# Weight loads on another engine's queue, and other constants in a planner that writes the order of a fused attention and feed-forward block

## The chip, the cores and the metric

The kernel runs on one core of one Trainium2 chip. Engines are named as the profile names them: PE is TensorE (PEld its weight loads), DVE is VectorE, ACT is ScalarE, POOL is GpSimd, SP is SyncE. Times are device microseconds. Three executions before the change took 1146.23, 1144.88 and 1145.27 us: median 1145.27. Less is better.

## The reference

The input x has 2 batches of 1024 tokens with 512 channels. With xn the layer norm of x over its channels:

```python
qkv = einsum('bsd,od->bso', xn, w_qkv) + b_qkv          # 32 heads of 16 channels
scores = q @ k.T / sqrt(16) + slope[head] * position[key]
scores = where(query >= key, scores, -1e9)
s = softmax(scores) @ v ; s = s @ w_out.T + b_out
gate, up = octonion_linear(xn, w_gate), octonion_linear(xn, w_up)    # weights cut to -scale, 0, +scale
g = silu(octonion_linear(silu(gate) * up, w_down))
out = x + s * g
```

An octonion linear layer multiplies 8 slices of the channels by 8 weight blocks, with the signs of an octonion product; the feed-forward part has 8 * 170 = 1360 hidden channels. The 1e9 mask, the softmax over 1024 keys and all sums are in float32.

## The kernel before, in words

The program has two stages. Attention fills the first 868 us of the profiled execution, the feed-forward part (`gate_up`, `down`) the rest; the change touches the first alone.

**Attention.** The 32 heads are worked on in 8 groups of 4, two groups to a pair. The work is cut into 32 *units* (batch, group, half of the queries). A *group (b, g)* below means the two units of batch b and group g. For each unit there are four kinds of steps:
- *Max scores* (`max_items`, L538): PE multiplies 128 queries by up to 512 keys into a tile of the PSUM pool `ps_x`, which has two buffers; DVE adds the mask to the diagonal block and takes the row's maximum. The names are `s1_...` in the program and `s` in the profile.
- *Placing the maxima* (`split_max`, `place_max`, L603): DVE splits the maxima in two parts, PE turns them, ACT copies them to `mr`, and two small DMAs from POOL write them into rows of the query tile `q_stack`, so that the next product subtracts them. The line of POOL is `q_stack<-mr`.
- *Exps* (`exp_step`, `exp_of`, L654 and L673): PE computes transposed scores into one of three buffers of `ps_e`, ACT takes the exponential into the SBUF tile `p`.
- *Values* (`value_step`, L692): PE multiplies `p` by `v`, four heads side by side; ACT copies the sum, PE turns it and DVE divides (`normalise`, L712), SP stores it.

Beside these there is *side work* on PE: projections to queries and keys (`qk_items`, L467), to values (`v_items`, L425), the output projection (`out_items`, L745 and L761) and, early on, transposes of tokens and of the down weights. Its results go through the pool `ps_m`, with two buffers. Queries and keys go out to DRAM and come back in another shape by DMAs of SP (`fill_q`, `fill_k`); they are the tiles `q_stack` and `k_stack`.

**The weights.** `load_wq` fetches the query and key weights of two groups, 512 KB in each of two DMAs, into `wqr`; `compact_wq` copies them together on POOL into `wq`. It is called once at the start and then late in each projection, for the next one (L475 to L477). `load_weight` fetches the gate, up and down weights in three DMAs each; gate was already on POOL, up and down on ACT. The DMAs of SP and of ACT take their completion semaphores in turn from the same eight (the order lists them as DMAHW0 to DMAHW7), those of POOL from eight others (DMASW0 to DMASW7). A DMA whose semaphore is still in use waits at its issue, and what stands behind it on that queue waits too.

**The planner.** `step` (L1261) writes the order of all engines by a list of costs. It keeps a clock for PE (`now`), one each for ACT and DVE (`run_act`, `run_dve`), and the time from which each PSUM buffer is free (`e_free`, `x_free`, `m_free`). `next_max`, `next_exp`, `next_turn`, `next_value`, `next_side` and `next_behind` each offer a next step with the time at which it can start; `step` takes one that can start soon, by priority. Side work has a due position in the units: past it, it has priority 3, before it priority 7, so that it is brought forward when nothing else is ready. Each cost is a number in nanoseconds in the code: from PE's end to the start of ACT or DVE 150, from their end until the buffer can be written again 60, an exp 510, a placing 3500 after ACT's copy. All steps are kept in the order that the planner writes, on every engine; once the attention stage is written, `held.clear()` gives the feed-forward part to the scheduler of the language.

Of the kernel before, what the change touches and what calls it, by code (L numbers as in the profile page):

```python
# [75 lines left out]
def kernel(  # L76
# [132 lines left out]
    act_.activation(warm, ones[:, 0:1], AF.Sqrt)  # L209
    for t in range(8):  # L210
        load_x(t, sp_)
    load_wq((0, 0), act_)
    load_wv(0)
    for n in range(2):
        for i in range(4):
# [235 lines left out]
    def qk_items(b, gp):  # L451

        box = {}

        def product(which, c, kt):
            if (which, c, kt) == (0, 0, 0):
                if (b, gp) not in wq_tiles:
                    compact_wq((b, gp))
                parts[b, gp] = [
                    spill.tile([2, P, S], F32, tag=f"sp{w}", name=f"sp_{b}_{gp}_{w}")  # L460
                    for w in range(2)
                ]
            if kt == 0:
                box["ps"] = ps_m.tile([P, 512], F32, tag="m", name=f"pqk_{b}_{gp}_{which}_{c}")
            ps = box["ps"]
            pe(
                nc.tensor.matmul(  # L467
                    ps,
                    lhsT=wq_tiles[b, gp][:, kt, which, :],
                    rhs=xnT[:, kt, b * S + c * 512 : b * S + (c + 1) * 512],  # L470
                    start=(kt == 0),
                    stop=(kt == KD - 1),
                )
            )
            n = b * NP + gp + 1  # L475
            if (which, c, kt) == (1, n > 1, KD - 1) and n < B * NP:
                load_wq((n // NP, n % NP), act_)  # L477
            if kt < KD - 1:
                return
            bias = bqk_sb[:, which, gp : gp + 1]  # L480
            st = stg.tile([P, 2, 512], F32R, tag="st", name=f"st_{b}_{gp}_{which}_{c}")
            act_.activation(st[:, 0, :], ps, AF.Identity, bias=bias)
            dve_.scalar_tensor_tensor(
                st[:, 1, :], ps, bias, st[:, 0, :].bitcast(F32), ALU.add, ALU.subtract
            )
            sp_.dma_start(
                out=parts[b, gp][which][:, :, c * 512 : (c + 1) * 512].rearrange(
                    "l p n -> p l n"
                ),
                in_=st.bitcast(F32),  # L490
            )

        return [
            (858, lambda w=w, c=c, kt=kt: product(w, c, kt), "qk" if kt == KD - 1 else None)
            for w in range(2)
            for c in range(2)
            for kt in range(KD)
        ]
# [415 lines left out]

    def load_later(w, name):
        later(
            lambda: load_weight(w, name, act_),
            lambda: set_known(("l", name), now[0] + 9000),
            ("k", name),
        )  # L920
# [103 lines left out]
    for t0 in (8, 12):  # L1024
# [18 lines left out]
        ("V", "R"): 200,  # L1043
        ("V", "F"): 100,
    }
    SOON = 80
    RUN = 1800
    HELD = 1e12
# [49 lines left out]
    def next_max(pos):  # L1098
        if M[0] == len(maxs):
            return []  # L1100
        u, n, count, heads_in, cost, diagonal, emit = maxs[M[0]]
        fill = 4 * (u // 2) + 1 + 2 * units[u][2]
        if fills[0] <= fill or n == 0 and u >= 2 and u - 2 not in placed:
            return []

        def go():
            emit()
            M[0] += 1
            run_pe("R", ready, heads_in * max(cost * 0.417 + 18, 108))
            end = run_dve(  # L1110
                now[0] + 150,
                heads_in * cost * 1.04 + 70 + (heads_in * 135 + 70) * diagonal,
            )
            take(x_free)[0] = end + 60
            if n == count - 1:
                split_max(*units[u], mtiles[u])
                turns.append((u, run_dve(end, 500) + 100))

        mpos = at[u] + (at[u + 1] - at[u]) * n / count
        lead = size[1] + size[0] * 0.6  # L1120
        ready = max(fill_at[fill], min(x_free))
        return [(ready, 4 if mpos < pos + lead else 5.5, 0, go)]

    def next_exp():
        if E[0] == len(exps):
            return []
        u, n, i, pieces = exps[E[0]]
        diagonal = n >= 4 * units[u][2]
        if u not in placed or V[0] < cells_at[u] + n - 2:
            return []  # L1130

        def after(ps):
            exp_of(*units[u], n, i, ps)
            end = run_act(now[0] + 150, 510)
            take(e_free)[0] = end + 60
            if i == (3 if len(pieces) == 1 or pieces[0][3] == 384 else 2):
                p_ready[cells_at[u] + n] = end + 60

        def go():
            ps = exp_step(*units[u], n, i, pieces)  # L1140
            E[0] += 1
            cost = sum(max(w * 0.417 + 18, 108) for _, _, _, w in pieces)
            run_pe("R", ready, cost + (60, 120)[len(pieces) - 1] * diagonal)
            after(ps)

        ready = max(placed[u] if n == 0 and i == 0 else 0, min(e_free))
        return [(ready, 5, 0, go)]

    def next_turn():
        found = []  # L1150
        if turns:
            u, t = turns[0]

            def go(u=u):
                turns.pop(0)
                place_max(*units[u], mtiles[u])
                run_pe("F", ready, 436)
                take(m_free)[0] = run_act(now[0] + 150, 500)
                placed[u] = m_free[0] + 3500

            ready = max(t, min(m_free))
            found.append((ready, 1, 0, go))
        if norms:
            u, t = norms[0]

            def go(u=u):
                norms.pop(0)
                normalise(*units[u])
                run_pe("F", t2, 436)
                take(m_free)[0] = run_dve(now[0] + 150, 600)  # L1170
                stored[units[u]] = m_free[0] + 5000

            t2 = max(t, min(m_free))
            found.append((t2, 2, 0, go))
        return [f for f in found if f[0] < HELD]

    def next_value():
        if V[0] == len(vals) or V[0] not in p_ready or not V[0] and S_[0] < head_v:
            return []
        u, n, cell = vals[V[0]]  # L1180
        last = 4 * units[u][2] + 2

        def go():
            value_step(*units[u], n, cell)
            V[0] += 1
            run_pe("V", ready, sum(w * 1.668 + 40 for _, _, w in cell))
            if n == last:
                o_free[0] = run_act(now[0] + 200, 500)
                norms.append((u, o_free[0] + 100))

        ready = max(p_ready[V[0]], o_free[0] if n == 0 else 0)

        if n % 2 == 0 and n < last and V[0] + 2 >= E_cell():
            ready = max(ready, p_ready.get(V[0] + 1, HELD) - 800)
        return [(ready, 0, 0, go)] if ready < HELD else []
# [7 lines left out]
    def next_side(pos):  # L1203
        if S_[0] == len(side):
            return []
        due, ok, (cost, emit, what, *need) = side[S_[0]]
        if not ok():
            return []

        def go():  # L1210
            emit()
            S_[0] += 1
            if cost:
                run_pe("F", ready, cost)
            if what == "none":
                return
            if HELD not in m_free:
                take(m_free)[0] = HELD
            if what is None:
                return  # L1220
            if what == "v":
                end = run_dve(now[0] + 150, 350)
            elif what == "qk":
                end = run_dve(run_act(now[0] + 150, 600), 700)
                done_qk[0] += 1

                if done_qk[0] == 2 or done_qk[0] % 4 == 0:
                    qk_done.append(end + 4000)
            elif what == "t":
                end = run_act(now[0] + 150, 500)  # L1230
            else:
                end = run_dve(now[0] + 150, 600)
            m_free[m_free.index(HELD)] = end + 60

        ready = 0 if HELD in m_free or not cost else min(m_free)
        for k in need:
            ready = max(ready, known[k] + 100)
        return [(ready, 3 if pos >= due else 7, cost, go)]

    def next_behind(pos):  # L1240
# [4 lines left out]
        def go():  # L1245
            behind.pop(0)
            emit()
            if model:
                model()
            if not cost:  # L1250
                return
            run_pe("F", ready, cost)
            if what == "t":
                take(m_free)[0] = run_act(now[0] + 150, 500)

        ready = known.get(need, 0) + 100
        if cost:
# [282 lines left out]
```

## Time and profile before

| | |
|---|---|
| Median of three runs | 1145.27 us |
| Profiled execution | 1146.23 us, of which span 1144.5 us |
| PE busy | 1066.6 us, 93% of the span |
| PEld busy | 702.4 us |
| DVE busy | 678.3 us, 59% |
| ACT busy | 506.7 us, 44% |
| POOL busy | 176.2 us, 15% |
| Granted clock of PE, mean | 0.975 |
| DMA queue q1 (SP and ACT) | 66336 packets, 87.48 MB |
| DMA queue q0 (POOL) | 3776 packets, 5.98 MB |

The chain of work that ended last is 73% PE, 11% DVE, 5% DMA and 4% ACT. A busy PE is not PE at its peak: matmuls are pipelined, their ends are modelled, and a matmul that waits inside its row counts as busy. Issuing a DMA is not counted as busy. A wait for several semaphores is put down to the one that came last. The slices of the page are 28.6 us each.

### The profile page before, as it was taken

How to read it: one execution, taken by the hardware profiler on the slowest of the kernel's cores; microseconds unless marked ns; L12 is line 12 of the kernel's file. 1: busy time of each engine (PE TensorE's matmuls, PEld its weight loads, DVE VectorE, ACT ScalarE, POOL GpSimd, SP SyncE). 2: the span in 40 equal slices, each digit the busy share in tenths (PEclk: the TensorE clock that was granted, in tenths of full speed). 3: DMA queues.
4: the chain of work that ended last, by engine and by line, in shares of the span. 5: the costliest groups of instructions: out<-in, count | busy, mean ns of one | idle time of the engine just before them, and what ended most of it. 6: DMA issues, size and time to landing. Idle time of an engine off the chain costs nothing.

```text
span 1144.5 us, 15617 instructions
## 1 busy us (share of the span) xinstructions
PE 1066.6 (93%) x5562; PEld 702.4 (61%) x5562; DVE 678.3 (59%) x1400; ACT 506.7 (44%) x962; POOL 176.2 (15%) x294
## 2 busy tenths in 40 slices
PE   7889969999998999999999999999879999999995
PEld 5554645675655666556566566565546687878783
DVE  5377786757777687777786877878531122131211
ACT  4122647654653634546536356356662123232321
POOL 6401023000111010100110000010001123242322
PEclk9899968999999999999999999999889999999998
DMA  6976463453745416442645154631041013030200
GB/s 194 204 140 153 108 168 83 59 80 112 145 114 129 72 31 124 130 86 43 138 65 76 66 113 99 137 62 42 17 143 65 33 42 111 1 111 1 77 34 37
DMA packets 73740, 104.24 MB, mean 91 GB/s; under 512 B 26992, under 2 KB 31120, under 8 KB 73664
## 3 DMA queue, kind: packets, MB, share of 16 engines
q1 hardware_dynamic: 66336, 87.48, 34.1%
q10 hardware_dynamic: 3552, 9.78, 2.6%
q0 software_dynamic: 3776, 5.98, 2.1%
q8 instruction: 45, 0.74, 0.3%
q14 instruction: 31, 0.25, 0.1%
HBM read 69.58 MB, written 33.10 MB: 90 GB/s over the span
## 4 chain that ended last, share of the span: by engine, by line
PE 73%; DVE 11%; DMA 5%; ACT 4%; issue 4%; POOL 1%; SPq 0%; ACTq 0%; DVEq 0%; POOLq 0%
PE s L538 13%; PE s L654 12%; PE po L692 11%; PE pg L1375 6%; PE pqk L467 6%; PE pu L1375 6%; PE pd L1409 5%; PE pout L761 4%; DVE mx L69 4%; PE s L673 3%; PE pv L425 3%; DMA q_stack<-mr 2%; DVE s L69 2%; ACT p L69 1%; DVE left L69 1%
## 5 line engine op out<-in xcount | busy, mean ns | idle before, releaser
L69 ACT ACTIVATE p<-s 128x512 f32<-128x512 f32 x576 | 309.9, 600 | 124.6 <-PE s L654 70.0
L538 PE MATMUL s<-k_stack,q_stack 126*128 126x512 f32 (+3 forms) x768 | 279.0, 417 | 24.0 <-DVE mx L69 16.2
L654 PE MATMUL s<-q_stack,k_stack 128*128 128x512 f32 (+3 forms) x768 | 229.0, 367 | 11.3 <-DMA q_stack<-mr 7.7
L69 DVE TENSOR_REDUCE mx<-s 128x1 f32<-128x384 f32 (+3 forms) x352 | 226.3, 643 | 11.7
L69 DVE TENSOR_REDUCE left<-s 128x1 f32<-128x512 f32 x256 | 169.2, 686 | 72.4 <-PE s L538 71.3
L538 PEld LDWEIGHTS s<-k_stack,q_stack 126*128 126x128 f32 x768 | 133.1, 194 | 119.0 <-PE s L538 35.7
L654 PEld LDWEIGHTS s<-q_stack,k_stack 128*128 128x128 f32 x768 | 140.8, 193 | 57.4 <-issue 18.5
L69 DVE TENSOR_TENSOR s<-s,mask 128x128 f32<-128x128 f32 (+2 forms) x352 | 124.2, 353 | 40.3 <-PE s L538 38.6
L692 PE MATMUL po<-p,v 128*32 128x512 f32 (+3 forms) x1536 | 140.5, 494 | 0.2 <-ACT p L69 0.2
L467 PE MATMUL pqk<-xnT,wq 128*128 128x512 f32 x256 | 129.4, 613 | 3.9 <-ACT xnT L69 2.0
L69 DVE SCALAR_TENSOR_TENSOR h<-pu,sc_u,sg 128x512 f32<-128x512 f32 (+1 forms) x44 | 33.0, 751 | 166.8 <-PE pu L1375 154.3
L69 POOL DMA_DIRECT2D q_stack<-mr x64 | 32.0, 505 | 603.3 <-ACT mr L69 603.3
L673 PE MATMUL s<-mask_r,ident_r 128*128 128x256 f32 (+1 forms) x320 | 89.2, 279 | 0.0
L69 POOL TENSOR_TENSOR hs<-h,hs 128x512 fp32r<-128x512 f32 (+1 forms) x44 | 57.5, 1307 | 197.9 <-ACT hs L69 197.8
L692 PEld LDWEIGHTS po<-p,v 128*32 128x32 f32 x1536 | 42.6, 110 | 73.0 <-issue 70.5
L69 ACT ACTIVATE sg<-pg,sc_g 128x512 f32<-128x512 f32 (+1 forms) x44 | 30.2, 687 | 100.5 <-PE pg L1375 95.6
L69 ACT ACTIVATE st<-pqk,bqk_sb 128x512 fp32r<-128x512 f32 x32 | 22.0, 688 | 118.2 <-PE pqk L467 102.3
L425 PE MATMUL pv<-wv,xnT 128*128 128x256 f32 x256 | 68.4, 386 | 1.9 <-DVE v L69 1.5
L467 PEld LDWEIGHTS pqk<-xnT,wq 128*128 128x128 f32 x256 | 48.2, 196 | 32.3 <-issue 22.0
L761 PE MATMUL pout<-wo_sb,oT 128*128 128x512 f32 x128 | 62.0, 606 | 1.4 <-ACT oT L69 1.0
L673 PEld LDWEIGHTS s<-mask_r,ident_r 128*128 128x128 f32 x320 | 60.9, 190 | 2.1
L69 ACT CAST hs<-h 128x512 fp32r<-128x512 f32 (+1 forms) x44 | 27.3, 619 | 75.8 <-DVE h L69 75.8
(143 smaller groups left out, 1100.4 us busy)
## 6 DMA issues: line engine op xcount, KB each, us to landing
sp<-st SPq DMA_DIRECT2D x32, 512.0 KB
k_stack<-sp SPq DMA_DIRECT2D x128, 128.0 KB
q_stack<-sp SPq DMA_DIRECT2D x128, 128.0 KB
wqr<-in_wqk_dram ACTq DMA_DIRECT2D x16, 512.0 KB
xt<-in_x_dram SPq DMA_DIRECT2D x16, 256.0 KB
att<-o SPq DMA_DIRECT2D x32, 128.0 KB
ot<-att SPq DMA_DIRECT2D x16, 256.0 KB
proj<-y SPq DMA_DIRECT2D x16, 256.0 KB
```

The costliest lines, as they stand in the source:

```text
L69: ins = issue(*args, **kwargs)
L425: nc.tensor.matmul(ps[:, 0:256], lhsT=xnT[:, c, b * S + kt * P : b * S + (kt + 1) * P], rhs=wv_tiles[2 * b + hh][:, c, :], start=(c == 0), ...
L467: nc.tensor.matmul(ps, lhsT=wq_tiles[b, gp][:, kt, which, :], rhs=xnT[:, kt, b * S + c * 512 : b * S + (c + 1) * 512], start=(kt == 0), st ...
L538: nc.tensor.matmul(ps[:, j * n : (j + 1) * n], lhsT=q_of(b, g, qc)[0 : NR - 2, first + j, tl * P : (tl + 1) * P], rhs=k_of(b, g, c)[0 : NR ...
L654: nc.tensor.matmul(ps[:, c0 : c0 + w], lhsT=k_of(b, g, kt // 4)[0:NR, h, kt % 4 * P : (kt % 4 + 1) * P], rhs=q[0:NR, h, 512 - w : 512], st ...
L673: pe(nc.tensor.matmul(out, lhsT=ident_r, rhs=rhs, start=False, stop=True))
L692: nc.tensor.matmul(po[32 * i : 32 * i + 32, 512 - w : 512], lhsT=v[:, kt, h * VC : h * VC + 32], rhs=p[:, i * part + c0 : i * part + c0 + ...
L761: nc.tensor.matmul(ps, lhsT=turned[t][:, c, :], rhs=wo_sb[0][:, c, :], start=(c == 0), stop=(c == KD - 1),)
L1375: nc.tensor.matmul(ps[:fs, :], lhsT=fw[mt][:, n0 + kt, 0:fs], rhs=part[:, kt, :], start=(kt == 0 and n == 0), stop=(kt == KD - 1 and n == 1),)
L1409: nc.tensor.matmul(pd, lhsT=hs[k][:fs, n, st * P : (st + 1) * P], rhs=fw[mt][:fs, 8:12, :].rearrange("p s n -> p (s n)"), start=(mt == 0 a ...
```

## The change

The issue of `load_wq` (16 DMAs) and of `load_weight` for up and down (6 DMAs) is moved from ACT to POOL. In the planner the lags from PE to ACT or DVE and back get names, START = 210 (150 before, 200 for the copy of the values' sum) and END = 160 (60 before, 100 after the last maximum of a unit and after the copy of the values' sum); an exp costs 485 in place of 510, the copy of the values' sum 480 in place of 500, and a placing 6000 in place of 3500. The planner writes another order from them: on PE, the changes between kinds of work (scores and exps, values, all else) go from 519 to 576, with the same 4451 matmuls.

```diff
@@ the start
-    load_wq((0, 0), act_)
+    load_wq((0, 0), pool_)
@@ qk_items, product
             if (which, c, kt) == (1, n > 1, KD - 1) and n < B * NP:
-                load_wq((n // NP, n % NP), act_)
+                load_wq((n // NP, n % NP), pool_)
@@ load_later
-            lambda: load_weight(w, name, act_),
+            lambda: load_weight(w, name, pool_),
@@ the planner
+    START, END = 210, 160
@@ next_max
             end = run_dve(
-                now[0] + 150,
+                now[0] + START,
                 heads_in * cost * 1.04 + 70 + (heads_in * 135 + 70) * diagonal,
             )
-            take(x_free)[0] = end + 60
+            take(x_free)[0] = end + END
             if n == count - 1:
                 split_max(*units[u], mtiles[u])
-                turns.append((u, run_dve(end, 500) + 100))
+                turns.append((u, run_dve(end, 500) + END))
@@ next_exp
-            end = run_act(now[0] + 150, 510)
-            take(e_free)[0] = end + 60
+            end = run_act(now[0] + START, 485)
+            take(e_free)[0] = end + END
             if i == (3 if len(pieces) == 1 or pieces[0][3] == 384 else 2):
-                p_ready[cells_at[u] + n] = end + 60
+                p_ready[cells_at[u] + n] = end + END
@@ next_turn
-                take(m_free)[0] = run_act(now[0] + 150, 500)
-                placed[u] = m_free[0] + 3500
+                take(m_free)[0] = run_act(now[0] + START, 500)
+                placed[u] = m_free[0] + 6000
...
-                take(m_free)[0] = run_dve(now[0] + 150, 600)
+                take(m_free)[0] = run_dve(now[0] + START, 600)
@@ next_value
-                o_free[0] = run_act(now[0] + 200, 500)
-                norms.append((u, o_free[0] + 100))
+                o_free[0] = run_act(now[0] + START, 480) + END
+                norms.append((u, o_free[0]))
@@ next_side
-                end = run_dve(now[0] + 150, 350)
+                end = run_dve(now[0] + START, 350)
             elif what == "qk":
-                end = run_dve(run_act(now[0] + 150, 600), 700)
+                end = run_dve(run_act(now[0] + START, 600), 700)
...
-            m_free[m_free.index(HELD)] = end + 60
+            m_free[m_free.index(HELD)] = end + END
```

In `next_side` and `next_behind` the other two 150s become START in the same way.

More of the change, by code (lines that the diff above doesn't have):

```diff
@@ L1229, in go @@
             elif what == "t":
-                end = run_act(now[0] + 150, 500)
+                end = run_act(now[0] + START, 500)
             else:
-                end = run_dve(now[0] + 150, 600)
-            m_free[m_free.index(HELD)] = end + 60
+                end = run_dve(now[0] + START, 600)
+            m_free[m_free.index(HELD)] = end + END
         ready = 0 if HELD in m_free or not cost else min(m_free)
@@ L1253, in go @@
             if what == "t":
-                take(m_free)[0] = run_act(now[0] + 150, 500)
+                take(m_free)[0] = run_act(now[0] + START, 500)
         ready = known.get(need, 0) + 100
```

## The prediction

> **What bounds the kernel now.** I read the slices first, then busy time by stage, then the waits, then single stretches of the timeline.
>
> ```profile
> span 1144.5 us, 15617 instructions
> ...
> PE   7889969999998999999999999999879999999995
> ...
> DVE  5377786757777687777786877878531122131211
> ...
> PEclk9899968999999999999999999999889999999998
> ```
>
> The busy times of three stretches (the stretch and its length, then busy time and instructions of PE, weight loads, DVE, ACT and POOL, then granted clock and DMA):
>
> ```profile
> 246.50:712.50 466.00, 451.07 (x2637) 280.86 (x2635) 352.72 (x739) 238.40 (x435) 33.08 (x76) 1.00 0.45 96
> 712.50:756.80 44.30, 43.67 (x261) 25.98 (x257) 35.30 (x76) 23.43 (x46) 2.00 (x4) 1.00 0.62 117
> 756.80:808.80 52.00, 46.85 (x269) 28.24 (x266) 43.43 (x101) 26.89 (x59) 3.87 (x5) 0.98 0.16 43
> ```
>
> PE is at 97% in the long middle (246.5 to 712.5, ten head groups from the first exp of group (0,3) to that of (1,5)), DVE at 76%, ACT at 51%. But a busy PE row holds waits too, as the group of the max scores shows (busy, mean ns, idle before and its releasers):
>
> ```profile
> L538 PE MATMUL s<-k_stack,q_stack 126*128 126x512 f32 (+3 forms) x768 | 279.0, 417 | 24.0 <-DVE mx L69 16.2 <-DVE left L69 3.3 <-DVE sc_d L69 0.8
> ```
>
> and the waits of PE and of SP's queue (total, times, longest):
>
> ```profile
> PE s L654 <- DMA q_stack<-mr: 7.7, 5, 3.3
> ...
> SPq L69 <- DMA wqr<-in_wqk_dram: 45.5, 6, 20.1
> ```
>
> I priced each matmul at its start-to-start time where nothing holds it (512 columns: scores and exps 0.231 us, a projection pair 0.858, four value matmuls 0.883) and added them in program order. The middle then needs 404 us of PE, and takes 466: 62 us are lost, 58 of them between one score or exp matmul and the next. 327 of 606 max-score tiles start within 0.2 us of the end of the DVE operation that frees their buffer. PE is the bound, with DVE's release of two score buffers behind every second tile. After 868 us comes the feed-forward part, which the change leaves alone.
>
> **The new constants against the trace.** Where DVE or ACT had been idle, it starts 0.20 us (median after transposes) to 0.26 us (median of 72 score tiles) after the last matmul's issue slot ends (the plan has 0.15, the change 0.21). Where PE waits for a score buffer, it starts 0.147 us after DVE's end (0.06, then 0.16). Exps in a row start 0.477 us apart (0.51, then 0.485). Placing, from the last transpose to the first exp, takes 3.8 to 8.2 us in the 17 units where the first exp follows at once; the plan allows the transfer 3.5, then 6.0. So the corrections are true. What counts is the order that they write.
>
> **The loads.** 22 issues (16 of query/key weights, 6 of feed-forward weights) leave ACT, at 0.434 us by the row of wqr: 9.5 us of an engine busy 44%, hidden behind PE. POOL takes them at about 0.6 us (w_g's row: 606 ns): 13 us of an engine busy 15%. SP loses the 45.5 us of waits above, and 8.5 more on the other two weights. Who waited for SP? No matmul in 62 to 830 us waited for a filled key or query tile; the order has the fills early enough. What SP's block did is to let fills out in a burst beside a placing:
>
> ```profile
> 356.13 0.82 ACTq L69 DMA_DIRECT2D wqr<-in_wqk_dram  x2
> 359.77 1.53 SPq L69 DMA_DIRECT2D k_stack<-sp  x2
> 362.60 1.02 POOL L69 DMA_DIRECT2D q_stack<-mr  x2 [29.02 <-ACT mr L69]
> 368.73 0.19 PEld L654 LDWEIGHTS s<-q_stack,k_stack 128*128 128x128 f32 x1 [2.57 <-DMA q_stack<-mr]
> ```
>
> The placing took 5.5 us here, against a median of 1.8, and another 4.9 us at 547 us, straight after a load. I count that under placing. On POOL the loads stand behind the previous placing, whose landing nobody on POOL awaits, so they go out some 10 to 20 us earlier; queued behind them are compactions, which need them anyway, and the next placing, which is held by two issues (1.2 us) at most if it comes just then. The load of w_d waits on POOL for DVE and a store; behind it stand the stores of the down weights, which need w_d too. The nearest row for harm is the 2.57 us above at one placing. I take 0, and keep -1 to +3. At the start POOL is 1.2 us later with its fills of zeros, but the first projection (17.5 us) waits for ACT: 0.
>
> The Trainium skill, DMA: Bandwidth & Descriptors, section "Issuing engines are not separate DMA queues", says that issuing from several engines saves only the sequencer's time to initiate a transfer. By it this half would be worth 9.5 us of ACT's idle time, so nothing. The SP row contradicts it in mechanism (SP stood 45.5 us), though not in the sum.
>
> **The order, middle.** I set the two listings of the order, of the program before and of the changed one, side by side, with the prices above. Total PE work up to the feed-forward part is equal (697 us). Terms from 246.5 to 712.5:
> - More side work (projections, transposes) is put early: the same stretch holds 414 us of PE in place of 404. +10.
> - Between a placing's transposes and its first exp, those 17 units have 0.8 to 4.6 us of PE work before (median 4.2), 2.3 to 7.2 after (median 6.4). The waits in the middle were 1.1, 2.6 and 1.7 us, and one brought 3.4 us at half clock (1.7 lost): -7.
> - Two-buffer shortfall of score tiles (lag 0.37 us plus DVE's time, less PE work in between, where positive) sums to 11.1 us before, 4.6 after: -6.5. For exps 4.9 and 1.9: -3.
>
> Sum -6.5. Bounds: nothing of the 16.5 is realised but the placing (+3), since sorted by that margin the measured loss per tile is nearly flat (0.14 us at 0.2 to 0.3 us, 0.15 at 0.75 to 1.0): DVE's queue, not seen by the margin, shares in it. Or half of the 58 us goes (-19).
>
> **The order, head** (62 to 246.5). Shortfalls go from 12.7 to 12.0 us for scores, from 0.6 to 2.3 for exps; the first placing left PE standing for some 3.5 us and now has 6.7 us of work before it instead of 3.9. I take -1, bounds -5 and +4: here 27 us run at half clock, which any shift can move.
>
> **The order, tail** (712.5 to 808.8, 96.3 us). 22 us of side work stood here, 12 are left, 3 of them from group (1,6) on. PE needs 78, then 68. DVE's work hardly changes: 78.7 us busy, 82%. It becomes the bound. At 87% it takes 90.7: -5.6. Bounds: 0 at today's share, -9.6 at 90%. Tiles whose margin is below -0.3 us go from 2 to 16 in the last three units; they measured 0.97 us lost each, and that is this DVE pace seen from PE, not a second price, unless PE's other work is held behind them: +8 at worst. Such a stretch also costs clock:
>
> ```profile
> 161.30:164.70 3.40, 1.86 (x12) 1.10 (x9) 3.30 (x7) 2.80 (x10) 1.29 (x2) 1.00 0.42 128
> 164.70:175.00 10.30, 9.02 (x27) 6.80 (x28) 7.18 (x18) 7.12 (x20) 3.89 (x6) 0.50 0.24 70
> ```
>
> PE at 55% of 3.4 us with DVE full, then 10.3 us at half clock. The tail had 6.8 us of that (at 806.4). I add 2 us, bounds 0 and 8, half of up to 16 us. The Trainium skill, TensorE: Matmul & The Clock Gate, Part 1, throttles after an idle window of about 3.4 us. By it no wait on DVE here (1.2 us at most) would cost clock, and this term would be 0; the rows decide against it.
>
> **Sum.** 0 - 1 - 6.5 - 5.6 + 2 = -11.1 us. Against the profiled execution's own 1146.23 us (span 1144.5 and 1.7 around it) 1135.1; it stood 0.96 above the median, so 1134.2 beside 1145.27.
>
> **The rivals.**
> - *Larger gain.* Truer lags remove half of the middle's 58 us, -29 in place of -9.5: 1115. For it: 327 just-in-time tiles. Against: two buffers and DVE at 76% leave little choice.
> - *The gain is given back.* Side work only moves forward: middle -6.5 as forecast, but a third of the 14 new short gaps is paid (14 x 0.97 / 3 = 4.5) in place of -5.6: -1 - 6.5 + 4.5 + 2 = -1, 1144. For it: equal PE work and the loss that is flat by margin.
> - *Slower: the tail starves.* Place: groups (1,5) to (1,7), side work gone one unit earlier. The middle keeps its loss but for the placing (+10 - 7 = +3), half of the new gaps is paid (6.8), clock 2, head -1: +10.8, 1156; with a quarter paid 1153. For it: all 14 gaps stand where nothing else is left to fill them. Against: PE has only 68 us of work in 96. With such a tail the kernel is slower if the middle's loss of 62 falls by less than about 14 us, with the forecast's tail only below 5.
>
> **How the numbers follow.** Forecast 0.47 (its own range 1127 to 1142, from the bounds of middle and tail taken half), larger gain 0.12, given back 0.14, slower 0.27. A change of 0.2% (2.3 us) is about what a measurement can tell from none. Faster: 0.47 + 0.12 and a little of the third, 0.61; same 0.12; slower 0.27. The range 1118 to 1154 leaves out most of the larger gain below and about half of the slower cases above, a fifth in all.
>
> **What would show it.** In the changed profile: no SP wait on wqr; POOL rows of wqr near 0.6 us; PE waits on placings below 3 us in total; the mean of the score matmul (417 ns) lower; the first exp of (1,5) near 705 us and of (1,7) near 797; DVE above 85% in between. Wrong if (1,5) starts after 715, or if the clock in the last 60 us of attention falls below 0.85.

## The result, and the profile after

The changed kernel takes 1148.64 us (median of 20 runs, 1142.30 to 1155.28), the kernel before 1146.24 us beside it (20 runs, 1144.54 to 1149.59): a ratio of 1.0022, 95% interval 1.0012 to 1.0033. It is slower by 2.4 us, where 11 us of gain were forecast. Its profiled execution took 1145.34 us, 3.3 us less than its median and 0.9 us less than the profiled execution before. So the traces can show where single stretches gained and lost; what separates the medians has to come from the experiments.

The page of the changed kernel:

```profile
span 1143.5 us, 15599 instructions
...
PE   7799969999999999999999999989879999999995
...
DVE  4288777777778777687786887778331122131211
...
PEclk9799969999999999999999999988889999999997
...
L538 PE MATMUL s<-k_stack,q_stack 126*128 126x512 f32 (+3 forms) x768 | 284.0, 424 | 27.6 <-DVE mx L69 20.7
```

Its busy times by stretch (stretch, length, then PE, weight loads, DVE, ACT, POOL, granted clock, DMA share, GB/s): the middle, from the first exp of group (0,3) to that of (1,5), and the tail from there to that of (1,7)'s first unit.

```profile
245.10:707.10 462.00, 451.24 (x2666) 285.20 (x2662) 352.30 (x739) 237.94 (x438) 37.45 (x84) 1.00 0.48 99
...
707.10:806.40 99.30, 88.51 (x496) 52.86 (x493) 79.75 (x182) 48.11 (x102) 5.89 (x9) 0.91 0.32 59
```

And three of its waits (total, times, longest):

```profile
PE s L538 <- DVE mx L69: 20.7, 43, 1.7
...
PE ptx L391 <- ACT xnT L69: 8.8, 1, 8.8
...
ACT st L69 <- DMA sp<-st: 5.0, 1, 5.0
```

SP's waits on `wqr` are gone, and so are PE's on placings (`q_stack<-mr`, 7.7 us before). The middle is 4.0 us shorter. The second slice from the left is lower on PE and DVE, the tail runs at clock 0.91 (0.99 before), and the mean of the score matmul rose from 417 to 424 ns. By stretches, in us:

| stretch | before | after | difference | forecast |
|---|---|---|---|---|
| to the first value projection | 43.2 | 48.8 | +5.6 | 0 |
| to the first exp of (0,0) | 35.7 | 34.7 | -1.0 | 0 |
| head, to the first exp of (0,3) | 167.6 | 161.6 | -6.0 | -1 |
| middle | 466.0 | 462.0 | -4.0 | -6.5 |
| tail | 96.3 | 99.3 | +3.0 | -3.6 |
| rest of attention | 58.0 | 57.0 | -1.0 | 0 |
| feed-forward part | 277.6 | 280.2 | +2.5 | 0 |

The last row is code that the change leaves alone. It took 277.6 to 281.6 us in the profiles of this study, with a half-clock stretch more or less near its end; it is taken as unexplained.

At the start a wait stands that nobody had in the kernel before. The timeline of the changed kernel (start, length, then in brackets the idle time before it and what ended it):

```profile
19.58 1.81 POOL L69 DMA_DIRECT2D w_g<-in_wg_dram  x3
...
21.38 1.16 POOL L69 DMA_DIRECT2D wqr<-in_wqk_dram  x2
...
22.52 1.80 POOL L69 DMA_DIRECT2D w_u<-in_wu_dram  x3
...
24.33 0.40 SPq L69 DMA_DIRECT2D sp<-st  x1
...
32.94 1.21 DVE L69 TENSOR_TENSOR al<-al_sb,al 32x1024 fp32r<-32x1024 f32 x1 [4.85 <-DMA sp<-st]
34.24 0.69 ACT L69 ACTIVATE st<-pqk,bqk_sb 128x512 fp32r<-128x512 f32 x1 [5.89 <-DVE al L69]
...
35.46 2.91 PE L391 MATMUL ptx<-ident,xt 128*128 128x128 f32 x12 [8.80 <-ACT xnT L69]
```

Eight loads (2.4 MB) go out within 5 us, and the store of the first projection, issued behind them at 24.33, holds the staging buffer `st` until 32.9. Before, w_u and the second `wqr` left at 33.4 and 27.8 us, and DVE took up the second position part `al` (the expectations call it the alibi part) at 28.42 without a wait.

### The profile page after: what moved, and what is told of

Read it like the earlier page. It is cut to its first block, busy times and chain, and to the rows that moved or that the text cites. A ratio compares the mean times of both kernels' runs of the same rounds, so it can differ in the third digit from the quotient of the medians.

```text
span 1143.5 us, 15599 instructions
## 1 busy us (share of the span) xinstructions
PE 1063.5 (93%) x5562; PEld 704.7 (62%) x5562; DVE 675.3 (59%) x1400; ACT 503.7 (44%) x962; POOL 189.0 (17%) x316
## 4 chain that ended last, share of the span: by engine, by line
PE 72%; DVE 13%; ACT 6%; issue 4%; DMA 3%; POOL 2%; SPq 0%; DVEq 0%; ACTq 0%; POOLq 0%
PE s L538 12%; PE s L654 11%; PE po L692 10%; PE pqk L467 8%; PE pg L1376 6%; PE pu L1376 6%; PE pd L1410 5%; DVE mx L69 5%; PE pout L761 4%; PE pv L425 3%; PE s L673 3%; DVE s L69 2%; ACT p L69 1%; PE pm L603 1%; DVE left L69 1%
## 5 line engine op out<-in xcount | busy, mean ns | idle before, releaser
L538 PE MATMUL s<-k_stack,q_stack 126*128 126x512 f32 (+3 forms) x768 | 284.0, 424 | 27.6 <-DVE mx L69 20.7
L692 PEld LDWEIGHTS po<-p,v 128*32 128x32 f32 x1536 | 42.8, 109 | 67.7 <-issue 64.9
```

What stands on the lines that cost most here:

```text
L538: nc.tensor.matmul(ps[:, j * n : (j + 1) * n], lhsT=q_of(b, g, qc)[0 : NR - 2, first + j, tl * P : (tl + 1) * P], rhs=k_of(b, g, c)[0 : NR ...
L692: nc.tensor.matmul(po[32 * i : 32 * i + 32, 512 - w : 512], lhsT=v[:, kt, h * VC : h * VC + 32], rhs=p[:, i * part + c0 : i * part + c0 + ...
```

## The experiments

Each ratio is to the kernel before on the same chip, with its 95% interval. "Loss" is a unit's length less PE's work in it at the prices of the prediction.

### The two halves

Loads alone, `e1`: only the three `act_` to `pool_` edits.

> The loads on POOL alone, with the old constants: PE, DVE and SP have the order of the kernel before. Theory 1 (the loads' burst at the start costs, the plan gains): the first value projection starts at 48.8 us in place of 43.2, DVE stands some 4.9 us before the second alibi part, and of these 5.6 us some 5 stay to the end: ratio about 1.004, 1151 us. Theory 2 (the loads are neutral over the whole kernel, the plan gives the time back): the 5 us are absorbed by slack in the head, or paid for by SP's 45.5 us of waits that go: ratio 0.999 to 1.001.

Constants alone, `e2`: all else of the change, the loads on ACT.

> The constants alone, with the loads on ACT: PE and DVE have the order of the changed kernel. Theory 1: the first value projection is back at 43.2 us, the middle keeps its gain, the tail its loss of 3 us: ratio 0.996 to 0.998, 1142 us. Theory 2: 1.002 or more, as the changed kernel; SP's waits on wqr are back at about 45 us.

Measured: loads alone 1148.93 us, 1.0015 (1.0000 to 1.0030); constants alone 1156.31 us, 1.0090 (1.0071 to 1.0109). The loads alone lie between the two theories; the constants alone fit the second ("1.002 or more"), but neither foresaw 0.9%. The halves don't add up: 0.15% and 0.90% alone, 0.22% together. With the constants alone PE loses 15.0 us in the second unit of (0,7), 2.6 before. Its timeline there:

```profile
430.85 26.30 SPq L69 DMA_DIRECT2D k_stack<-sp  x4
...
451.58 0.82 ACTq L69 DMA_DIRECT2D wqr<-in_wqk_dram  x2
...
460.77 0.36 SPq L69 DMA_DIRECT2D sp<-st  x1
...
466.57 0.69 ACT L69 ACTIVATE st<-pqk,bqk_sb 128x512 fp32r<-128x512 f32 x1 [14.45 <-DMA sp<-st]
...
467.30 0.75 DVE L69 SCALAR_TENSOR_TENSOR st<-pqk,bqk_sb,st 128x512 fp32r<-128x512 f32 x1 [11.59 <-ACT st L69]
...
468.99 0.77 PE L538 MATMUL s<-k_stack,q_stack 126*128 126x512 f32 x1 [11.62 <-DVE mx L69]
```

The wait of SP's queue in 425 to 462 us of the same run:

```profile
SPq L69 <- DMA wqr<-in_wqk_dram: 24.6, 2, 24.1
```

This is a chain through four engines that comes back to ACT. ACT issues the load at 451.58, behind its copies. SP's fills of `k_stack`, begun at 430.85, stand until that load lets the shared semaphore go; behind them on SP stands the store `sp<-st` (460.77); ACT's next copy needs the buffer that this store empties and waits 14.45 us; DVE behind ACT 11.59, PE 11.62, and PE's clock is at half for 13.7 us, from 459.0, inside that wait, to 472.6. The changed kernel's same four fills take 2.92 us (428.62). So the loads on POOL are worth some 8 us in the new order (1156.3 to 1148.6).

### The start

The changed kernel with `load_wq` of the second pair and w_u on ACT again, `e3`, and repeated on another chip, `e15`:

```diff
-                load_wq((n // NP, n % NP), pool_)
+                load_wq((n // NP, n % NP), pool_ if n > 1 else act_)
-            lambda: load_weight(w, name, pool_),
+            lambda: load_weight(w, name, act_ if name == "u" else pool_),
```

> The changed kernel, but the two loads of the first 25 us (query/key weights of the second group pair and w_u) issued by ACT again, as before. Theory 1: DVE's wait before the second alibi part falls from 4.85 us to below 1, the first value projection starts at about 43.5 us and the end comes some 5 us earlier than in the changed kernel: ratio 0.997 to 0.999. Theory 2: the start is 5 us earlier too, but the head takes it back by clock or by waits on fills: ratio 1.001 to 1.003.

> The run with the start loads back on ACT once more, as the control on this chip: ratio near 1.000, runs 1142 to 1151 us apart, ACT's wait for the staging buffer at 70 to 83 us between 5 and 12 us, the first unit's length 28.2 us of work and that wait longer or shorter with it.

The second position part in another buffer, `e4`:

```diff
-            home, tag = (stg, "st") if n else (wop, "wo")
+            home, tag = (pp, "p") if n else (wop, "wo")
```

> The changed kernel, but the second alibi part goes to a buffer of the probabilities' pool and no longer waits for the store of the first projection. The burst of loads stays. If that buffer is the whole of the start's loss: DVE's idle of 4.85 us goes, first value projection near 43.5 us, ratio 0.997 to 0.999. If the burst itself is (every transfer of the start is late), the first max score, which waits for stores and fills, stays near 55 us and the ratio near 1.002.

Measured: `e3` 1147.64 us, 1.0005 (0.9990 to 1.0021), `e15` 1147.26, 1.0008 (0.9995 to 1.0021); the first value projection at 42.8 and 44.0 us. `e4` 1149.78 us, 1.0023 (1.0004 to 1.0041), at 47.8 us. In `e4` DVE's wait is gone, and the burst's is not:

```profile
25.59 0.38 SPq L69 DMA_DIRECT2D sp<-st  x1
...
29.38 1.21 DVE L69 TENSOR_TENSOR al<-al_sb,al 32x1024 fp32r<-32x1024 f32 x1
...
33.20 0.69 ACT L69 ACTIVATE st<-pqk,bqk_sb 128x512 fp32r<-128x512 f32 x1 [3.59 <-DMA sp<-st]
```

The store itself takes 7.6 us to let its buffer go, and now ACT waits for it directly. So the burst delays the store, and which tile shares the buffer matters little. But undoing it gave back only 1.0 us of median (1.0005 and 1.0008 for 1.0022; the intervals overlap, and `e3` lies between its two theories): of the 6.0 us between the traces of the changed kernel and of `e3` at the first value projection 1.9 are left at the second unit of (0,0) (112.6 us before, 116.3 changed, 114.4 in `e3`).

### The late loads alone

The kernel before with the loads on POOL but for these two, `e8`, and repeated, `e16`. With w_u on POOL as well, `e11`.

> The kernel before with its loads on POOL except the two of the first 25 us. If the burst at the start is the loads' only harm: first value projection at 43.2 us as before, the 4 us of placing waits and the half clock near 370 us stay gone, ratio 0.997 to 0.999. If the burst's 5 us are absorbed anyway and the loads' harm lies elsewhere: 1.001 to 1.002, as with all loads on POOL.

> The late loads alone once more, on this chip: ratio near 0.998, runs within 4 us of each other, no ACT wait on a store at 70 to 83 us.

> The late loads on POOL with the plan of the kernel before, and of the two start loads w_u on POOL too (issued near 22 us in place of 33), the query/key weights still on ACT at 28 us. If w_u makes the burst: the store of the first projection lands late, the first value projection starts at 45 to 49 us, and the median rises by 3 to 6 us: ratio 1.000 to 1.003. If the query/key weights do: 43.2 us and 0.998.

Measured: `e8` 1142.70 us, 0.9978 (0.9965 to 0.9990), and `e16` 1142.02 us, 0.9965 (0.9951 to 0.9978). This version beats both kernels. `e16` and `e15` ran on the same chip with the same loads and differ by the constants alone: 1142.02 against 1147.26 us, so the new constants cost 5.2 us there, and the intervals are apart. `e1` differs from `e8` by the two start loads alone: with the old order these cost 4 to 6 us of median (1.0015 against 0.9978 and 0.9965). Its trace, at 1142.93 us 6 us short of its median, doesn't show where.

The middle and tail of `e8`:

```profile
244.50:706.90 462.40, 449.82 (x2637) 279.42 (x2635) 352.26 (x739) 238.64 (x435) 37.56 (x84) 1.00 0.45 97
706.90:803.20 96.30, 90.73 (x525) 54.26 (x522) 78.72 (x177) 50.40 (x105) 5.89 (x9) 0.98 0.37 77
```

With the old order the middle falls from 466.0 to 462.4 us: the loss of (0,5)'s first unit goes from 5.6 to 3.0 us and that of (1,1)'s from 5.4 to 3.6, the two places where the prediction had seen a placing held by SP's burst of fills; the 3.4 us of half clock at 369.5 go too. `e11` took 1146.26 us, 1.0000 (0.9986 to 1.0013), with its first value projection at 43.9 us. So w_u alone makes no late start, but the median lies 0.2% above that of `e8`; where, its one trace doesn't show (span 1142.7 us, `e8`'s 1140.8).

### The constants one by one

Longer lags and shorter exps without the longer placing, `e5`; the longer placing alone, `e6`, both with all loads on POOL; and on `e8` the shorter exps alone, `e12`.

> The changed kernel, but the plan allows 3.5 us for a placing again: what is left of the plan's half are the longer lags and the shorter exps. In its order group (1,6)'s first unit still has no side work (12.3 us of PE work in it, 12.8 in the changed kernel, 18.7 in the kernel before). If the lags' pulling of side work out of the end is the cause: that unit again takes 24 to 26 us with about 10 us at half clock, and with some placing waits back (the loads on POOL already took most of them) the ratio is 1.003 to 1.006. If the longer placing is: the unit takes 22 us and the ratio is 0.998 to 1.000.

> The loads on POOL and the longer placing alone, with the old lags and exp times. Its order leaves 6.9 us of side work in the first unit of group (1,6), as in the kernel before. If the lags empty the end: that unit takes 22 us as before, no half clock there, the start still 5 us late and mostly regained by 113 us, ratio 0.997 to 1.000. If the longer placing is what the changed kernel pays for: 1.003 or more.

> The late loads on POOL, and of the plan's corrections only the shorter exps (485 for 510 ns, 480 for 500). It changes the order in 20 of 32 units by 1 to 3 us of side work each, and the shortfall of score tiles hardly (18.7 us before, 17.5 after in (0,1) to (1,7)). If truer numbers write a better order, each by itself: ratio below 0.998. If any new order is a new draw against the one that the kernel before has (longer placings alone and longer lags alone were both slower than both together): anywhere between 0.997 and 1.006, by single stalls that can be named in its trace.

Measured: `e5` 1152.47 us, 1.0055 (1.0040 to 1.0070); `e6` 1154.70 us, 1.0079 (1.0055 to 1.0104); `e12` 1144.90 us, 0.9988 (0.9974 to 1.0003). The same loads with the old constants have 1.0015 (`e1`) beside `e5` and `e6`, and 0.9978 and 0.9965 (`e8`, `e16`) beside `e12`. `e5`'s first unit of (1,6) takes 22.9 us, 9.9 of them at half clock; it loses more at (0,3) (7.8 us for 1.5) and (0,7). `e6` keeps its tail (21.4 us in that unit), as expected, and is yet the slowest of the three: its trace loses 11.2 us in the first unit of (1,4), where PE stands 5.5 us for a row of `att` that SP fetches late (`pot` waits on `ot<-att`) and the clock is at half for 6.8 us from 693.2 on, within that wait. That trace is of its slowest run, 1160.64 us. All three corrections are true by the trace of before, and none of these runs shows a gain from one; longer lags without shorter exps were not run. Each writes another order, and the traces show other single losses, the largest from 5 to 15 us, some of them on resources that the planner has no price for: staging buffers, SP's queue, fetched rows.

### The tail

`e3` with the output projection of batch 0 held for units of (1,3) to (1,6), `e7`:

```diff
+            if b == 0:
+                for k in range(len(side) - len(its), len(side)):
+                    j = k - len(side) + len(its)
+                    side[k] = (
+                        side[k][0],
+                        lambda ok=side[k][1], u=[[22, 22, 24], [26, 28, 28]][n][j // 8]: ok() and unit_of(exps, E[0]) >= u,
+                        side[k][2],
+                    )
```

> The changed kernel with the two start loads back on ACT (as in the run that moved these back), and the output projection of batch 0 may not start before units (1,3), (1,4), (1,5) and (1,6), a part in each. In its order the first unit of (1,6) has 18.3 us of PE work in place of 12.8, and the shortfall of score tiles from (1,4) to (1,7) goes from 19.4 to 13.9 us. If the emptied end is the cause: that unit takes 20 to 22 us in place of 25.4, the half clock near 761 us goes, and the whole is 4 to 7 us below the run with the start loads back: ratio 0.995 to 0.997. If a PE that waits for DVE there is only one of several such places (units (1,4) and (1,5) lose what (1,6) gains): ratio 1.000 to 1.001.

`e3` with empty matmuls behind the score tiles of (1,6)'s first unit, `e9`, and `e8` with such in (0,1)'s first unit, `e10` (then `u in (2,)`):

```diff
+    def fill_up():
+        u = unit_of(exps, E[0])
+        if u in (28,) or u - 1 in (28,) and u not in placed:
+            t = ps_m.tile([P, 512], F32, tag="m", name=f"fill_{M[0]}")
+            pe(nc.tensor.matmul(t[:, 0:256], lhsT=ones, rhs=mask[0:64, 0:256], start=True, stop=True))
...
             emit()
+            fill_up()
```

> The run with the start loads back on ACT, and 17 empty fp32 matmuls of 256 columns (0.43 us each at full clock, 7.3 us) put behind the score tiles of the first unit of (1,6), nothing else moved: they compute nothing that is used. If what the emptied end costs is the clock (PE starved, then half speed): the half clock near 761 us goes, the unit falls from 25.4 to about 22 us, as it was with 5.9 us more of useful work, and the whole gains about 3 us: ratio 0.997 to 0.999. If DVE's pace alone sets the unit: it stays at 25 us or grows by what the empty matmuls hold up, ratio 1.001 to 1.005.

> The late loads on POOL with the plan of the kernel before, and 21 such empty matmuls (9.0 us) behind the score tiles of the first unit of group (0,1), which takes 35 us for 17.5 us of PE work with 14 us at half clock. If the clock is the price there: the half clock of 150 to 171 us shrinks, the unit falls to about 29 us, ratio 0.992 to 0.995. If DVE and ACT set its pace (the signs of the feed-forward weights are made there): the unit stays at 35 us or grows by up to 9, ratio 0.998 to 1.006.

Measured: `e7` 1146.62 us, 1.0000 (0.9980 to 1.0021). The first unit of (1,6) is mended (loss 3.9 us for 12.6, no half clock), and (1,4) and (1,5) pay: their first units lose 5.1 and 8.4 us for 3.0 and 4.0, and from the first unit of (1,4) to that of (1,7) the loss is 42 us, `e3`'s 41. The expected rival holds. `e9` 1147.45 us, 1.0026 (1.0004 to 1.0048): the unit grew from 25.4 to 30.7 us, though its half clock fell from 11.7 to 2.7 us. `e10` 1157.36 us, 1.0095 (1.0077 to 1.0113): 47.8 us for 34.9, with 17.1 us at half clock for 14.1. The empty matmuls stood ahead of the next score tile on PE:

```profile
773.22 0.50 PE L538 MATMUL s<-k_stack,q_stack 126*128 126x512 f32 x1
...
773.65 0.70 PE L1103 MATMUL fill<-mask,ones 64*128 64x256 f32 x2
...
774.28 0.50 PE L538 MATMUL s<-k_stack,q_stack 126*128 126x512 f32 x1
```

A tile every 1.06 us, where DVE alone needs 0.93. They made PE the pace, so these two runs don't separate the clock from DVE's pace; they show that work on PE isn't free in a stretch that waits for DVE. DVE's own timeline in the changed kernel does more:

```profile
763.38 0.29 DVE L69 TENSOR_TENSOR s<-s,mask 128x128 f32<-128x128 f32 x1
763.70 0.69 DVE L69 TENSOR_REDUCE mx<-s 128x1 f32<-128x512 f32 x1
764.31 0.29 DVE L69 TENSOR_TENSOR s<-s,mask 128x128 f32<-128x128 f32 x1
...
768.49 1.29 DVE L69 TENSOR_REDUCE left<-s 128x1 f32<-128x512 f32 x2 [0.41 <-PE s L538]
770.38 0.70 DVE L69 TENSOR_TENSOR s<-s,mask 128x512 f32<-128x512 f32 x1 [0.61 <-PE s L538]
...
772.76 1.29 DVE L69 TENSOR_REDUCE left<-s 128x1 f32<-128x512 f32 x2 [0.35 <-PE s L538]
774.34 0.69 DVE L69 TENSOR_REDUCE left<-s 128x1 f32<-128x512 f32 x1 [0.29 <-PE s L538]
```

While PE is at full clock, DVE's tiles follow without a gap (0.93 us). From 764.9 on PE is at half clock, a score tile takes twice its time, and DVE waits for PE, 1.7 us in these four rows. The unit is 3.4 us longer than before: 2.6 us are DVE work that the order moved into it (20.0 us for 17.4), the rest is DVE's idle time, 5.3 us for 4.5.

### A wait that the first traces hid

In the kernels with the changed order, ACT's copy of the third projection piece of pair (0,1) stands ahead of the first exps and waits for a staging buffer: 5.0 us in the changed kernel, 7.8 in `e3`, 11.6 in `e9`, and in these three the loss of the unit goes with it (4.6, 7.8, 12.2 us). The kernel before is no better there: its unit takes 33.7 us, 32.8 in the changed kernel, and its fourth copy has such a wait (5.62 us, until 97.09). `e13` is `e3` with that piece's last matmul after the first exps, as in the order before; `e14` has `e7`'s edit too.

```diff
-    lead_in += [(size[0] + 4 * d, None, it) for d, it in zip(due[::2], qk_items(0, 1))]
+    lead_in += [
+        (size[0] + 4 * d, None if n < 11 else lambda: E[0] >= 6, it)
+        for n, (d, it) in enumerate(zip(due[::2], qk_items(0, 1)))
+    ]
```

> The run with the start loads back on ACT, and in the plan the last matmul of the third projection piece of (0,1) (and all side work behind it) may not be put before 6 exps of the first unit are. ACT's copy of it then stands behind the first exps, as in the kernel before. If the wait for the staging buffer is what the profiles of the changed kernel miss: no ACT wait on that store at 70 to 83 us, the first unit takes 32 to 34 us, and the runs come 3 to 5 us below the same kernel without the edit and closer together: ratio 0.997 to 0.998. If the emptied end is the cause: 1.000 to 1.001, as without it.

> The same, and the output projection of batch 0 held for the last units as in the run with the side work held. If both matter: 5 to 8 us below the changed kernel, ratio 0.994 to 0.996. If the held side work only moves the loss from (1,6) to (1,4) and (1,5): as the run with the third piece alone, 0.997 to 0.998.

The third copy in `e9` and in `e13`, from ACT's timeline of each:

```profile
82.46 0.69 ACT L69 ACTIVATE st<-pqk,bqk_sb 128x512 fp32r<-128x512 f32 x1 [11.59 <-DMA sp<-st]
```

```profile
89.99 0.69 ACT L69 ACTIVATE st<-pqk,bqk_sb 128x512 fp32r<-128x512 f32 x1 [0.81 <-PE pqk L467]
```

The wait goes and the unit takes 32.4 us, as expected, but the time does not follow: `e13` 1147.33 us, 1.0012 (0.9996 to 1.0028); `e14` 1147.12 us, 1.0005 (0.9989 to 1.0021); `e15`, unmended on the same chip, 1147.26. Neither expectation for `e14` holds. The new order takes 5.4 us more loss in (0,3)'s second unit (7.3 us for 1.9). The wait is real, and by these runs it is not what the medians differ by.

What they differ by stays open. The profiled runs of `e15` and `e16` took 1141.09 and 1141.08 us, and their medians are 1147.26 and 1142.02. Of 12 runs of `e15` two are near 1141 and ten from 1146 to 1150. Within most kernels the longer runs have the lower mean clock (changed kernel: correlation -0.77 over 20 runs; 1142.3 us at 0.971, 1155.3 at 0.964), and the kernels with the changed constants and no burst have a mean of 0.967 (`e3`, `e15`), the late loads alone 0.976 and 0.977. An estimate from it: 0.010 of 1145 us less clock is 23 us more at half speed, up to 11 us of PE work, enough for the difference. But the runs speak against the clock as the whole cause. `e14` has a mean clock of 0.975, as the kernel before has on the same chip, and yet 1147.12 us, no less than `e15` with 0.967; and the profiled executions of the two kernels have 0.975 before and 0.966 after, though the second is the shorter one. Where in the program the typical run loses its time, no trace taken shows.

## Why the prediction was wrong

The forecast was 1134.2, -11.1 us; measured +2.4 us of median, -0.9 us in the trace. The range holds the time; the direction was wrong, and slower had the chance 0.27. The step that failed is the worth of the new order: -11.1 us of terms, the tail's above all, and the loads put at 0. With the late loads on POOL in both, the new order measured +5.2 us of median (`e15` against `e16`), while the profiled executions of these two took the same time. By the traces the tail failed most, +3.0 for -3.6; where the rest of the median goes stays open.

- **The loads, 0 (bounds -1 to +3).** This step failed twice. "At the start ... the first projection (17.5 us) waits for ACT: 0" looked at POOL's fills and not at what the early transfers share the DMA engines with: the store at 24.33. That was +5.6 us in the trace at the first value projection; to the end it was 1 to 2 us of median with the new order and 4 to 6 with the old one. And "Who waited for SP? No matmul" was read from the order before and used for the new one, where the loads on ACT would have cost 8 us (`e2` against the whole change) by the chain through SP, ACT and DVE. The late loads alone are worth -2.5 to -4.0 us (0.9978, 0.9965). With the old order the whole half measured +1.7 (1.0015), within the bounds because the two errors cancel.
- **Placing, -7, counted for the plan.** The waits went, to 0. But 3.6 us of the middle's gain come with the late loads alone and the old placing; the longer placing alone made a slower kernel (1.0079, beside 1.0015 with the same loads).
- **Middle, -6.5.** Right in kind. 413 us of work stand where 404 stood (10 forecast, 9 found), and the loss fell from 62 to 49 us: 13.1 of 16.5. Length -4.0. On top of the late loads the plan gives 1.5 (460.9 in `e3`, 462.4 in `e8`).
- **Tail, -5.6 and +2 for the clock.** The term that failed by most, 6.6 us: +3.0. "At 87% it takes 90.7" had no row behind it (and 78.7 us at 87% are 90.5, at 90% 87.4, which is -8.9 and not -9.6); DVE was at 82% and is at 80% (79.75 of 99.3). The bound "0 at today's share" was nearest. The loss of side work left DVE's pace where it was, added 1 us of DVE work to the stretch and 13.7 us of half clock.
- **Head, -1 (bounds -5 to +4).** -6.0 in the trace, which made good the late start; -2.4 in `e3` and +3.2 in `e9`, with the staging wait of the third piece. No step of the working priced ACT's wait for a store, which the plan can't see either.
- **The rivals.** "The gain is given back" came nearest to the trace (-1 us for -0.9), by luck: its tail is +6.5 for the +3.0 measured, and the late start and the faster head are not in it. "The tail starves" named the right place and missed the middle, which kept its gain. That each half could be slower alone was not among them.

Of the signs named beforehand: no SP wait on `wqr`, POOL's rows at 0.55 us and no placing wait above 3 us came true, (1,5) starts at 707 for 705; the score matmul's mean rose, (1,7) starts at 806 for 797, DVE is at 80% for 85. The sign against it, a clock below 0.85 in the last 60 us of attention, did not show as worded (0.92 from 806.4 to 863.4); the clock fell earlier, to 0.84 over the last 56 us of the tail.

The rule on issuing engines that the prediction weighed (the Trainium skill, DMA: Bandwidth & Descriptors, "Issuing engines are not separate DMA queues") gave nothing for this half. The runs disagree: the late loads' engine alone is worth 0.2 to 0.35%, because an issue that waits in one engine's order holds the DMAs of another. The burst at the start doesn't contradict it: a store of SP's queue was late beside loads of POOL's.

## What to carry to other kernels

Side work brought forward fills one stall and opens another: list what is left for each later stretch, and take the pace of the engine behind it from a row, not from a hoped-for share. Ask of every in-order queue in the new order, not in the old one, what stands behind a DMA that has to wait, and through which buffers that comes back. Truer constants in a planner are not a gain by themselves: under the same loads no order that they wrote here was faster than the old one (`e5`, `e6`, `e12`, `e15`). That each is only a new draw among orders, until the planner also prices staging buffers and SP's queue, is my reading and not shown. And where a change is worth 0.2%, one profile (3 to 6 us off the median here) doesn't decide it.

## What the hardware showed that was not expected

A PE that is partly busy can lose its clock. In the changed kernel's tail (the stretches are 3.4, 3.4 and 13.7 us):

```profile
758.10:761.50 3.40, 3.20 (x36) 1.62 (x28) 1.45 (x4) 1.07 (x3) 0.53 (x1) 1.00 0.00 0
761.50:764.90 3.40, 1.23 (x3) 0.45 (x3) 3.30 (x11) 0.00 (x0) 0.00 (x0) 0.99 0.35 67
764.90:778.60 13.70, 11.28 (x28) 6.77 (x28) 11.66 (x24) 2.22 (x5) 1.00 (x2) 0.50 0.04 14
```

PE is busy for 1.23 of 3.4 us, no wait there is longer than 1.71 us, and 13.7 us at half clock follow. In `e9`, with the empty matmuls, the same place held full clock at 3.21 of 3.4 us and lost it after 1.82 of 3.4. The Trainium skill (TensorE: Matmul & The Clock Gate, Part 1) asks for an idle window of about 3.4 us; here less than that was enough. The busy share alone doesn't decide it either: in `e12` 1.56 of 3.4 us (from 796.7) and in the changed kernel 1.90 of 3.41 (from 201.66) kept full clock. What does is open.

A store of 512 KB let its buffer go 8.6 us after its issue (24.33 to 32.94) with 2.4 MB of loads beside it; before, DVE had that buffer by 28.42, at most 3.8 us after the issue at 24.63.
